# Second attention of a two-layer transformer: matmuls in the order written, rotation halves copied by ACT, one masked maximum for a row's last tile, and 28 instead of 17 units whose maxima DVE subtracts

## The chip, the cores and the metric

One core of a Trainium2 chip. The metric is the device time of one execution in microseconds. The five engines run independent queues, each in order: PE (TensorE, matmuls), DVE (VectorE), ACT (ScalarE), POOL (GpSimd) and SP (SyncE, which issues all DMAs here).

## The reference

Two layers, each attention and a mixture-of-experts FFN, on x of shape (2, 1024, 128), float32. The change lies in the second layer's attention, and a little in the FFN that follows. Shortened:

```
x = x + L0_attn(layernorm(x)); x = x + L0_ffn(layernorm(x))      # 16 heads of 8; 8 experts, top 2
h = layernorm(x)                                                  # second attention:
q = (h @ Wq) -> 8 heads of 128;  k = (h @ Wk), v = (h @ Wv) -> 4 heads of 128
q = q * cos + rotate_half(q) * sin;  k = k * cos + rotate_half(k) * sin
attn = softmax(where(causal, -inf, q @ k.T / sqrt(128)))          # two q heads share one kv head
x = x + (attn @ v).reshape(b, t, 1024) @ Wo
x = x + L1_ffn(layernorm(x))                                      # RMS norm inside, 16 experts, top 4
```

`rotate_half` puts the negated second half of the 128 head dimensions in front of the first half.

## The kernel before

The kernel runs five stages after one another on the one core: first attention (`attn0`), its FFN, second attention (`attn1`), its FFN (`ffn1_back`). The framework's scheduler orders each engine's instructions by a timeline it computes while building; only the first attention marks PE as scheduled by hand (`manual_schedule(engines={PE})`), which means that PE's queue is the order in which the program issues the matmuls.

The second attention works on 32 **units** (batch b, kv head, query chunk qc of 256 rows), numbered 16 b + 4 kv + qc. Three generators feed it:

- `attn1_proj` makes K, Q and V of one (b, kv): per half of 512 rows one K projection, two Q projections (three matmuls each, `mm3`, because values are split into a high and a low float32r part) and two V projections of six narrower matmuls (with Wo already folded in). K and Q pass through `rope`: DVE makes A = p * cos (`rA`) and the two halves of B = swapped p * sin (`rB`) straight from PSUM, POOL adds them, ACT casts the high part, POOL subtracts to get the low part.
- `attn1_s` finds the row maxima for the softmax ahead of its use: for each of a unit's two row tiles and two heads, PE makes scores `s` in tiles of up to 512 keys (PSUM pool `a1s`, three buffers). DVE reduces what lies wholly below the diagonal (`pm`, L838, and L840 where there are two tiles), then adds the causal mask to the last 128 columns and takes the maximum in the same instruction (L844). At the unit's end PE transposes the four columns of maxima (`mt`, L848). The maxima are rows now, and are taken off the transposed scores in one of two ways. For units in `APART` (17 of 32) ACT copies the rows, SP writes them to DRAM (`md`, L853) and reads them back broadcast to 128 partitions (`mb`, L854), and DVE subtracts (L883). For the others DVE builds `mr` (L859) and PE subtracts with a further matmul, the **row matmul** (L880).
- The main loop in `attn1` walks the units; a unit has 2 qc + 2 **steps** (kt), 20 for each (b, kv) and 160 in all. A step makes transposed scores `st` of 128 keys against 256 queries of both heads (three matmuls, L873; half as wide in a unit's last step), subtracts the maxima, takes the exponential on ACT into `pt` (L885, four buffers), and in a unit's last two steps POOL zeroes what lies above the diagonal (L889). Then `attn1_av` multiplies with V into `o` (L906; a 129th column of ones gives the softmax's sum). At the end of a row tile DVE takes the reciprocal (`rz`), ACT scales, POOL adds into x.

The loop issues the `o` of a step after the `st` of the next. `s` and projections are issued between, by fixed counts of steps (13 tiles of `s` ahead at the start, 28 for 20 steps; ten projections for 20 steps, all in the first twelve). `st`, projections, `mt` and other transposes share a PSUM pool of three buffers (`pt`). Side work (`Side`): layer norms and transposes of the second batch, weights of the last FFN, and `ffn1_front` (norm, gating, top-k) of chunks 0, 1 and 2, one generator step for each attention step.

Of the kernel before, what the change touches and what calls it, by code (L numbers as in the profile page):

```python
# [20 lines left out]
D = 128  # L21
# [3 lines left out]
CH = 512  # L25
# [8 lines left out]

APART = (3, 4, 6, 7, 12, 14, 15, 18, 21, 22, 24, 26, 27, 28, 29, 30, 31)
INV_SQRT_D = 1.0 / float(D) ** 0.5
# [36 lines left out]
class Net:  # L73
# [481 lines left out]
    def topk(self, sc, k, E, name):  # L555
        nc = self.nc
        n = sc.shape[1]
        idx = self.idx[:, 0:E].unsqueeze(1).to_broadcast([128, n, E])
        s1 = self.small.tile([128, n, 1], F32, tag="tk1", name=f"tk1_{name}")
        eq = self.small.tile([128, n, E], F32, tag="tk2", name=f"tk2_{name}")  # L560
        work = self.small.tile([128, n, E], F32, tag="tk3", name=f"tk3_{name}")
        sel = self.small.tile([128, n, E], F32, tag="tk4", name=f"tk4_{name}")
        first = self.small.tile([128, n, 1], F32, tag="tk5", name=f"tk5_{name}")
        for i in range(k):
            cur = sc if i == 0 else work
            m = first if i == 0 else s1
            nc.vector.tensor_reduce(m, cur, AX.X, ALU.max)
            nc.vector.tensor_tensor(eq, cur, m.to_broadcast([128, n, E]), ALU.is_equal)
            nc.vector.tensor_mul(eq, eq, idx)
            nc.vector.tensor_reduce(s1, eq, AX.X, ALU.max)  # L570
            nc.vector.tensor_tensor(eq, eq, s1.to_broadcast([128, n, E]), ALU.is_equal)
            if i + 1 < k:
                nc.vector.scalar_tensor_tensor(work, eq, -3.0e38, cur, ALU.mult, ALU.add)
            if i == 0:
                nc.vector.tensor_copy(sel, eq)
            else:
                nc.vector.tensor_add(sel, sel, eq)
            yield
        return sel, first
# [133 lines left out]
    def attn1_weights(self, ctx):  # L713
# [4 lines left out]
        self.sin = wp.tile([128, T], F32, name="sin")  # L718
        self.cmask = wp.tile([128, 128], F32, name="cmask")
        self.bmask = wp.tile([4, 4, 1], F32, name="bmask")  # L720
# [47 lines left out]
    def rope(self, dst, p, i, name):  # L768
        nc, wk = self.nc, self.a1r
        cs = cols(i, CH)  # L770
        A = wk.tile([128, CH], F32, tag="rA", name=f"rA_{name}", bufs=2)
        Bt = wk.tile([128, CH], F32, tag="rB", name=f"rB_{name}")
        nc.vector.tensor_mul(A, p, self.cos[:, cs])
        nc.vector.tensor_mul(Bt[0:64], p[64:128], self.sin[64:128, cs])
        nc.vector.tensor_mul(Bt[64:128], p[0:64], self.sin[0:64, cs])  # L775
        nc.gpsimd.tensor_add(A, A, Bt)
# [39 lines left out]
    def attn1_s(self, kvt, b, kv, qc, res):  # L816
# [3 lines left out]
        for t in range(2):  # L820
            qt = 2 * qc + t
            n = (qt + 1) * 128
            for h in range(2):
                col = m[:, 2 * h + t : 2 * h + t + 1]
                ini = -3.0e38
                for k0 in range(0, n, CH):
                    k1 = min(n, k0 + CH)
                    s = self.a1s.tile([128, CH], F32, tag="s", name=f"s_{b}_{kv}_{h}_{qt}_{k0}")
                    with ExitStack() as ctx:
# [4 lines left out]
                        )  # L834
                    w = min(n - 128, k1) - k0
                    if w > 0:
                        pm = self.small.tile([128, 1], F32, tag="pm", name=f"pm_{b}_{kv}_{h}_{qt}_{k0}")
                        nc.vector.tensor_reduce(pm, s[:, 0:w], AX.X, ALU.max)  # L838
                        if k0 > 0:
                            nc.vector.tensor_max(pm, pm, ini)  # L840
                        ini = pm
                    if k1 == n:
                        d = s[:, n - 128 - k0 : n - k0]
                        k = nc.vector.tensor_tensor_reduce(d, d, self.cmask, 1.0, ini, ALU.add, ALU.max, col)  # L844
                        self.marks["V"] = k
                    yield
        tp = self.pt([4, 128], f"mt_{b}_{kv}_{qc}")
        nc.tensor.transpose(tp, m, self.ident)  # L848
        if self.rows_apart(b, kv, qc):
# [5 lines left out]
            res[(b, kv, qc)] = mb  # L855
            yield
            return
        r = wk.tile([4, 4, 128], F32R, tag="mr", name=f"mr_{b}_{kv}_{qc}", bufs=3)
        nc.vector.tensor_mul(r, self.bmask.to_broadcast([4, 4, 128]), tp.unsqueeze(1).to_broadcast([4, 4, 128]))  # L859
        res[(b, kv, qc)] = r  # L860
        yield

# [58 lines left out]
    def attn1(self, first, first_gen, xh, side_plan):  # L921
# [23 lines left out]
        def s_stream():  # L945
            for b, kv, qc in units:
# [3 lines left out]
                yield from self.attn1_s(kvts[(b, kv)], b, kv, qc, mres)  # L950

        ps = proj_stream()
        next(ps)
        ss = s_stream()
        lead = 0
        lag = []
        step = 0
        for u, (b, kv, qc) in enumerate(units):
            for g in side_plan.get(u, ()):
                extra.add(g())  # L960
            kvt = kvts[(b, kv)]
            while (b, kv, qc) not in mres:
                next(ss)
                lead += 1
            mr = mres.pop((b, kv, qc))
            acc = {}
            for kt in range(2 * qc + 2):
                e = self.attn1_st(kvt, b, kv, qc, kt, mr)
                step += 1
                while lead < 13 + step * 28 // 20:  # L970
                    next(ss, None)
                    lead += 1
                k, r = divmod(max(step - 3, 0), 20)
                want = min(5, 2 * step) + 10 * k + (min(10, r * 10 // 12 + 1) if step >= 3 else 0)
                while sum(pdone.values()) - 5 < want:
                    if next(ps, 1) == 1:
                        break
                extra.step()
                lag.append((kvt, b, kv, qc, kt, e, acc))
                if len(lag) > 1:  # L980
                    self.attn1_av(*lag.pop(0))
        for args in lag:
            self.attn1_av(*args)
        extra.drain()

# [30 lines left out]

    def ffn1_front(self, c):
        nc = self.nc
        E = 16
        x = self.x[c]  # L1020
        assert self.nx[("a1", c)] == 16
        mv = yield from self.stats([x[:, t, :] for t in range(TPC)], f"f1_{c}")
        v = self.small.tile([128, 2 * TPC], F32, tag="f1v", name=f"f1v_{c}")
        nc.vector.tensor_scalar(v[:, 0:TPC], mv[:, :, 1], 1e-5, None, ALU.add)
        nc.vector.scalar_tensor_tensor(v[:, TPC:], v[:, 0:TPC], 1e-5, mv[:, :, 1], ALU.mult, ALU.add)
        rs = self.rsqrt(v, 2 * TPC, f"f1_{c}")
        yield
        xl = self.tok.tile([128, TPC, D], F32, tag="xl", name=f"f1xl_{c}")
        tt = self.tok.tile([128, TPC, D], F32, tag="xn", name=f"f1tt_{c}")
        for t in range(TPC):  # L1030
            for dst, j in ((tt, TPC + t), (xl, t)):
                nc.vector.tensor_scalar(
                    dst[:, t, :], x[:, t, :], mv[:, t, 0:1], rs[:, j : j + 1], ALU.subtract, ALU.mult
                )
            yield
        nc.gpsimd.tensor_add(x, x, xl)
        tp = self.pt([128, CH], f"f1tp_{c}")
        self.transposes(tp, tt)
        xT = self.tok.tile([128, CH], F32, tag="xT", name=f"f1T_{c}")
        nc.scalar.mul(xT, tp, self.f1sc)  # L1040
        yield
        xh = [self.hl.tile([128, CH], F32R, tag=f"fh{k}", name=f"f1x{k}_{c}", bufs=3) for k in range(2)]
        self.split(xh, xT)
        yield
        lg = self.pt([128, TPC, E], f"f1lg_{c}")
        for t in range(TPC):
            nc.tensor.matmul(lg[:, t, :], lhsT=xT[:, cols(t)], rhs=self.f1gw, start=True, stop=True)
        g = self.small.tile([128, TPC, E], F32, tag="f1g", name=f"f1g_{c}")
        nc.vector.tensor_add(g, lg, self.f1gb.unsqueeze(1).to_broadcast([128, TPC, E]))
        yield  # L1050
        sel, mx = yield from self.topk(g, 4, E, f"f1_{c}")
        nc.vector.tensor_sub(g, g, mx.to_broadcast([128, TPC, E]))
        nc.scalar.activation(g, g, AF.Exp)
        nc.vector.tensor_mul(g, g, sel)
        self.normalise(g, E, f"f1_{c}")
        yield
        gp = self.pt([E, CH], f"f1gp_{c}")
        self.transposes(gp, g)
        gT = self.hl.tile([E, CH], F32, tag="fgT", name=f"f1gT_{c}", bufs=3)
        nc.scalar.copy(gT, gp)  # L1060
        gd = self.dram.tile([E, CH], F32, tag="f1gd", name=f"f1gd_{c}", bufs=4)
        nc.sync.dma_start(out=gd, in_=gT)
        self.f1st[c] = (xh, gT, gd)
        yield

# [74 lines left out]
def build(tc, aps, upto=4):  # L1140
# [7 lines left out]
    with ExitStack() as ctx:  # L1148
# [35 lines left out]
        with ExitStack() as c2:  # L1184
            with ExitStack() as c3:
# [14 lines left out]
                if upto > 3:  # L1200
                    plan[9] = [lambda: held(n, weights1())]
                    plan[18] = [lambda: n.ffn1_front(0)]
                    plan[21] = [lambda: n.ffn1_front(1)]
                    plan[30] = [lambda: later(n.ffn1_front(2), 3)]
# [11 lines left out]
def layout(inputs):  # L1216
# [31 lines left out]
    o["cos"] = np.concatenate([np.cos(ang), np.cos(ang)], axis=1).T.astype(np.float32)  # L1248
    o["sin"] = np.concatenate([np.sin(ang), -np.sin(ang)], axis=1).T.astype(np.float32)
    o["cmask"] = np.triu(np.full((128, 128), -1.0e38, np.float32), 1)  # L1250
    o["bmask"] = -np.eye(4, dtype=np.float32)[:, :, None]
# [29 lines left out]
```

## Time and profile before

| what | value |
|---|---|
| runs | 969.1, 977.7, 968.48 us; median 969.1 |
| profiled execution | 963.49 us, its span 961.7 |
| PE clock granted, mean | 0.991 |
| busy in the span | PE 924.5, DVE 824.9, ACT 597.7, POOL 314.7 us |
| busy from 500 to 850 us (second attention) | PE 344.1, DVE 310.5, ACT 166.3 us |
| second attention, first `st` to last `o` | 469.5 to 847.6 us |

Busy time counts from an instruction's start to its end as the profile has them. Instructions of one engine overlap at their ends, matmuls most, so that a busy share near 100% doesn't say that nothing more fits. "Idle before ... <- X" in a line names what released the engine after it had waited. A name such as `pt<-st,mb` says which tile is written from which.

### The profile page before, as it was taken

The page shows a single profiled execution, that of the slowest core. Times are in us where ns is not written, and L with a number is a line of the kernel's source. Part 1 is how long each engine was busy: PE and PEld are TensorE (multiplying, and loading weights), DVE is VectorE, ACT ScalarE, POOL GpSimd, SP SyncE. Part 2 cuts the span into 40 slices and gives each one's busy share as a digit, 9 for nine tenths or more (in the row PEclk, how much of TensorE's full clock was granted, in tenths as well). Part 3 has the DMA queues.
Part 4 walks back from the last instruction along what each step waited for, and adds up shares of the span by engine and source line. Part 5 has one row for each costly group of instructions (what it writes and reads, how often), then busy time and mean ns, then how long its engine had stood idle before and what let it go on. Part 6 is the DMA issues. An engine that isn't in the chain of part 4 may idle for free.

```text
span 961.7 us, 17534 instructions
## 1 busy us (share of the span) xinstructions
PE 924.5 (96%) x6554; PEld 608.8 (63%) x6554; DVE 824.9 (86%) x1793; ACT 597.7 (62%) x1160; POOL 314.7 (33%) x392
## 2 busy tenths in 40 slices
PE   7999999999999999999899999999999999998997
PEld 4544444444444444567678888787878789876675
DVE  7998789989998989557688978899989898899986
ACT  3178788888887878853344455444445445577785
POOL 9002100000100000022564657364646365336332
PEclk8999999999999999999999999999999999999999
DMA  6620530011010000042000001000000000154462
GB/s 177 197 78 1 167 120 1 1 45 48 16 31 1 1 1 2 2 132 68 1 1 23 13 21 56 12 13 12 13 12 13 13 12 34 35 165 153 154 195 70
DMA packets 33127, 50.80 MB, mean 53 GB/s; under 512 B 4693, under 2 KB 10802, under 8 KB 33042
## 3 DMA queue, kind: packets, MB, share of 16 engines
q1 hardware_dynamic: 33042, 49.68, 16.2%
q8 instruction: 51, 0.84, 0.4%
q14 instruction: 34, 0.28, 0.1%
HBM read 40.00 MB, written 9.67 MB: 52 GB/s over the span
## 4 chain that ended last, share of the span: by engine, by line
PE 67%; DVE 19%; ACT 8%; issue 4%; POOL 0%; DMA 0%; DVEq 0%; ACTq 0%; POOLq 0%
PE av L427 12%; PE st L407 11%; PE o L906 9%; PE st L873 8%; ACT pt L413 3%; PE s L832 3%; PE st L880 3%; PE av L374 2%; PE f0y L702 2%; DVE mx L368 2%; DVE pm L838 2%; PE f1y L163 2%; PE hot L374 2%; DVE pt L883 2%; PE f1p L163 2%
## 5 line engine op out<-in xcount | busy, mean ns | idle before, releaser
L368 DVE TENSOR_REDUCE mx<-s 128x2 f32<-128x1024 f32 x256 | 300.3, 1218 | 28.4 <-PE s L363 23.8
L413 ACT ACTIVATE pt<-st 128x512 f32<-128x512 f32 x476 | 253.4, 602 | 43.6 <-PE s L363 33.9
L427 PE MATMUL av<-pt,V 128*32 128x256 f32 x2048 | 159.3, 392 | 0.0
L906 PE MATMUL o<-V,pt 128*128 128x129 f32 x1152 | 156.8, 277 | 0.7 <-ACT pt L885 0.7
L906 PEld LDWEIGHTS o<-V,pt 128*128 128x128 f32 x1152 | 146.8, 191 | 12.8 <-issue 3.9
L363 PE MATMUL s<-KS,QM 24*128 24x512 f32 x512 | 152.0, 496 | 2.1 <-DVE mx L368 1.6
L407 PE MATMUL st<-QX,KS 25*128 25x512 f32 x476 | 144.2, 495 | 3.8 <-ACT pt L413 2.3
L873 PE MATMUL st<-Q,K 128*128 128x512 f32 (+1 forms) x480 | 133.2, 389 | 4.9 <-DVE rB_q L775 3.4
L407 PEld LDWEIGHTS st<-QX,KS 25*128 25x128 f32 x476 | 63.0, 182 | 98.8 <-ACT pt L413 46.0
L456 POOL TENSOR_TENSOR x<-x,ov 128x128 f32<-128x128 f32 x16 | 7.3, 455 | 331.8 <-DVE ov L453 331.8
L885 ACT ACTIVATE pt<-pt 128x512 f32<-128x512 f32 x92 | 53.8, 592 | 73.4 <-DVE pt L883 73.4
L838 DVE TENSOR_REDUCE pm<-s 128x1 f32<-128x512 f32 (+3 forms) x160 | 80.7, 522 | 16.9 <-PE s L832 16.0
L873 PEld LDWEIGHTS st<-Q,K 128*128 128x128 f32 x480 | 78.8, 189 | 16.6 <-DVE rB_q L775 4.7
L427 PEld LDWEIGHTS av<-pt,V 128*32 128x32 f32 x2048 | 42.9, 108 | 63.5 <-issue 59.2
L885 ACT ACTIVATE pt<-st 128x512 f32<-128x512 f32 x68 | 37.5, 551 | 62.8 <-PE st L880 51.7
L363 PEld LDWEIGHTS s<-KS,QM 24*128 24x128 f32 x512 | 65.6, 182 | 10.4 <-DVE mx L368 6.7
L832 PE MATMUL s<-K,Q 128*128 128x512 f32 (+2 forms) x192 | 66.4, 379 | 2.8 <-DVE m L844 2.7
L919 POOL TENSOR_TENSOR x<-x,w 128x128 f32<-128x128 f32 x128 | 59.5, 465 | 24.7 <-ACT w L917 20.4
L883 DVE TENSOR_TENSOR pt<-st,mb 128x512 f32<-128x512 f32 x92 | 57.5, 631 | 5.0 <-PE st L873 1.5
L163 PE MATMUL f1y<-f1s,f1w 128*128 128x512 f32 x192 | 55.1, 406 | 5.8 <-POOL f1s L159 3.5
L917 ACT ACTIVATE w<-o,rz 128x128 f32<-128x128 f32 x128 | 39.9, 364 | 33.2 <-DVE rz L913 25.4
L889 POOL TENSOR_SCALAR_AFFINE_SELECT pt<-pt 128x256 f32<-128x256 f32 x64 | 26.4, 415 | 91.9 <-ACT pt L885 90.1
(228 smaller groups left out, 1594.1 us busy)
## 6 DMA issues: line engine op xcount, KB each, us to landing
f1gb<-f1gd SPq DMA_DIRECT2D x64, 256.0 KB
mb<-md SPq DMA_DIRECT2D x17, 256.0 KB
f0gb<-f0gd SPq DMA_DIRECT2D x32, 128.0 KB
kd<-k SPq DMA_DIRECT2D x12, 256.0 KB
qd<-q SPq DMA_DIRECT2D x12, 256.0 KB
QM<-qd SPq DMA_DIRECT2D x3, 1024.0 KB
KS<-kd SPq DMA_DIRECT2D x2, 1024.0 KB
KS<-kd SPq DMA_DIRECT2D x2, 768.0 KB
```

The source lines that it names most:

```text
L163: self.nc.tensor.matmul(out, lhsT=lhs[l], rhs=rhs[r], start=start and i == 0, stop=stop and i == 2)
L363: self.last_s = nc.tensor.matmul(ps[:, k, :], lhsT=QM[c][r, g, cols(t)], rhs=KS[c // 2][r, g, cols(h, CH)], start=True, stop=True)
L368: self.marks["V"] = nc.vector.tensor_reduce(mxs[n][:, h, 2 * pr : 2 * pr + 2, t : t + 1], ps, AX.X, ALU.max, negate=True)
L407: nc.tensor.matmul(ps, lhsT=KS[c // 2][32 * j : 32 * j + 25, g, cols(kt)], rhs=QX[n][32 * j : 32 * j + 25, :], start=True, stop=True,)
L413: self.marks["A"] = nc.scalar.activation(e, ps, AF.Exp, scale=INV_SQRT_D)
L427: return nc.tensor.matmul(avs[n][cols(j, 32), q], lhsT=V[c // 2][kt // 4][:, kt % 4, 4 * g + j, :], rhs=es[j][:, q], start=kt == 0 and i = ...
L832: nc.tensor.matmul(s[:, 0 : k1 - k0], lhsT=Q[0][:, h, cols(qt)], rhs=K[0][:, k0:k1], start=True, stop=True)
L838: nc.vector.tensor_reduce(pm, s[:, 0:w], AX.X, ALU.max)
L873: k = nc.tensor.matmul(o, lhsT=K[l][:, cols(kt)], rhs=Q[r][:, :, q0 : q0 + w], start=i == 0, stop=apart and i == 2)
L883: nc.vector.tensor_sub(e[:, :, 256 - w :], o, mv)
L885: k = nc.scalar.activation(e[:, :, 256 - w :], o, AF.Exp, scale=INV_SQRT_D)
L906: nc.tensor.matmul(acc[t][:, h, :], lhsT=e[:, h, cols(t)], rhs=V[:, kt, h, :], start=(kt == 0 and h == 0), stop=(kt == qt and h == 1),)
```

## The change

1. The second attention's matmuls are issued under `manual_schedule(engines={PE})`: PE's queue is the program's order. The transpose of a unit's maxima and what follows it move out of `attn1_s` into `attn1_rows`, which is called two steps after the unit's last `s` (`due1`), or at once when the unit's first step comes before that.
2. `rope`: ACT copies the two halves of the projection from PSUM into `rB`, exchanged; DVE then multiplies `rB` by a sine table with its signs changed, in one instruction and in place.
3. `attn1_s`: DVE reduces only whole tiles of 512 that another follows. The last tile of a row, 128 to 512 columns, is masked and reduced in one instruction, with a mask of 512 columns of which the right part is used.
4. `APART` becomes all units but every eighth (28 of 32): only the fourth chunk of the odd kv heads keeps the row matmul.
5. `ffn1_front` takes several chunks. Chunks 0 and 1 are done together, begun at unit 18 (before: at 18 and at 21).

```diff
-APART = (3, 4, 6, 7, 12, 14, 15, 18, 21, 22, 24, 26, 27, 28, 29, 30, 31)
+APART = tuple(u for u in range(32) if u % 8 != 7)
 ...
-        self.cmask = wp.tile([128, 128], F32, name="cmask")
+        self.cmask = wp.tile([128, CH], F32, name="cmask")
 ...
+        nc.scalar.copy(Bt[0:64], p[64:128])
+        nc.scalar.copy(Bt[64:128], p[0:64])
         nc.vector.tensor_mul(A, p, self.cos[:, cs])
-        nc.vector.tensor_mul(Bt[0:64], p[64:128], self.sin[64:128, cs])
-        nc.vector.tensor_mul(Bt[64:128], p[0:64], self.sin[0:64, cs])
+        nc.vector.tensor_mul(Bt, Bt, self.sin[:, cs])
         nc.gpsimd.tensor_add(A, A, Bt)
 ...
-                    w = min(n - 128, k1) - k0
-                    if w > 0:
-                        pm = self.small.tile([128, 1], F32, tag="pm", name=f"pm_{b}_{kv}_{h}_{qt}_{k0}")
-                        nc.vector.tensor_reduce(pm, s[:, 0:w], AX.X, ALU.max)
-                        if k0 > 0:
-                            nc.vector.tensor_max(pm, pm, ini)
-                        ini = pm
-                    if k1 == n:
-                        d = s[:, n - 128 - k0 : n - k0]
-                        k = nc.vector.tensor_tensor_reduce(d, d, self.cmask, 1.0, ini, ALU.add, ALU.max, col)
+                    if k1 < n:
+                        ini = self.small.tile([128, 1], F32, tag="pm", name=f"pm_{b}_{kv}_{h}_{qt}_{k0}")
+                        nc.vector.tensor_reduce(ini, s, AX.X, ALU.max)
+                    else:
+                        d = s[:, 0 : n - k0]
+                        mask = self.cmask[:, CH - (n - k0) :]
+                        k = nc.vector.tensor_tensor_reduce(d, d, mask, 1.0, ini, ALU.add, ALU.max, col)
                         self.marks["V"] = k
                     yield
+        self.due1[self.step1 + 2].append(lambda: self.attn1_rows(m, b, kv, qc, res))
+        yield
+
+    def attn1_rows(self, m, b, kv, qc, res):
+        nc, wk = self.nc, self.a1k
         tp = self.pt([4, 128], f"mt_{b}_{kv}_{qc}")
         nc.tensor.transpose(tp, m, self.ident)
 ...
+        def tick():
+            for f in self.due1.pop(self.step1, ()):
+                f()
+            self.step1 += 1
 ...
+        with self.tc.manual_schedule(engines={PE}):
 ...
                 while (b, kv, qc) not in mres:
-                    next(ss)
-                    lead += 1
+                    if self.due1:
+                        tick()
+                    else:
+                        next(ss)
+                        lead += 1
                 mr = mres.pop((b, kv, qc))
                 acc = {}
                 for kt in range(2 * qc + 2):
                     e = self.attn1_st(kvt, b, kv, qc, kt, mr)
 ...
+                    tick()
                     extra.step()
                     lag.append((kvt, b, kv, qc, kt, e, acc))
                     if len(lag) > 1:
                         self.attn1_av(*lag.pop(0))
 ...
-    def ffn1_front(self, c):
+    def ffn1_front(self, *cs):
 ...
-                    plan[18] = [lambda: n.ffn1_front(0)]
-                    plan[21] = [lambda: n.ffn1_front(1)]
+                    plan[18] = [lambda: n.ffn1_front(0, 1)]
 ...
-    o["sin"] = np.concatenate([np.sin(ang), -np.sin(ang)], axis=1).T.astype(np.float32)
-    o["cmask"] = np.triu(np.full((128, 128), -1.0e38, np.float32), 1)
+    o["sin"] = np.concatenate([-np.sin(ang), np.sin(ang)], axis=1).T.astype(np.float32)
+    o["cmask"] = np.triu(np.full((128, 512), -1.0e38, np.float32), 385)
```

## The prediction

> **What bounds the kernel now.** I read the page's first part, then the second attention alone (469.5 to 847.6 us, first score matmul `st` to last output matmul `o`), cut by windows at the eight (batch, kv head) pairs, then the costliest groups there, the timeline of a few steps, and last the order in which the built programs list each engine's instructions.
>
> ```profile
> PE 924.5 (96%) x6554; PEld 608.8 (63%) x6554; DVE 824.9 (86%) x1793; ACT 597.7 (62%) x1160; POOL 314.7 (33%) x392
> ```
> ```profile
> 469.50:523.50 54.00, 51.70 (x301) 41.13 (x302) 44.56 (x117) 23.97 (x49) 29.95 (x37) 1.00 0.03 11
> ...
> sum 378.10, PE 370.25 PEld 305.86 DVE 333.22 ACT 178.60 POOL 204.77; mean PE 46.28 PEld 38.23 DVE 41.65 ACT 22.33 POOL 25.60
> ```
> The columns are the stretch, its length, busy time (instructions) of PE, weight loads, DVE, ACT and POOL, PE's clock, and DMA. In these 378.1 us PE is busy 98%, DVE 88%, ACT 47%, POOL 54%. PE sets the end, DVE is close behind. Because matmuls overlap, I price PE by the distance from one start to the next. The chain of waits gives 0.70 for the three wide `st` matmuls (0.233 per 512 columns), 0.70 for a K or Q projection, 0.71 for a V projection, 0.89 for eight `o` records (0.11 each). The timeline gives the row matmul L880, which subtracts a unit's maxima on PE:
>
> ```profile
> 606.09 0.87 PE L873 MATMUL st<-Q,K 128*128 128x512 f32 x3
> 606.88 0.49 PE L880 MATMUL st<-mr,ones_r 4*128 4x512 f32 x1
> 607.30 0.50 PE L832 MATMUL s<-K,Q 128*128 128x512 f32 x1
> ```
> From `st` to what follows the row it is 1.21, so a wide row costs 1.21 - 0.70 = 0.51, a narrow one 0.12 less (379 against 494 ns in the groups), about 0.40. Priced so, everything PE does in the stage is st 101, o 127, s 33, projections 52, rows 33, the rest 6: 352 us. So PE loses only 26 of 378 us, although DVE is nearly full. The scheduler gets this by placing a step's `o` late: the median from last `st` (or row) matmul to first `o` is 4 to 5 us.
>
> The row path of a unit with subtraction on DVE is seen in the last unit, `st` being the step's scores:
>
> ```profile
> 830.37 0.27 PE L848 MATMUL mt<-ident,m 128*4 128x128 f32 x1
> 831.01 0.24 ACT L851 COPY mb<-mt 4x128 f32<-4x128 f32 x1
> 831.27 0.25 SPq L853 DMA_DIRECT2D md<-mb  x1
> 832.48 0.34 SPq L854 DMA_DIRECT2D mb<-md  x1
> 835.70 1.29 DVE L883 TENSOR_TENSOR pt<-st,mb 128x512 f32<-128x512 f32 x2 [0.42 <-DMA mb<-md]
> 836.42 1.29 ACT L885 ACTIVATE pt<-pt 128x512 f32<-128x512 f32 x2 [4.45 <-DVE pt L883]
> 836.45 1.68 PE L873 MATMUL st<-Q,K 128*128 128x512 f32 x6 [1.16 <-DVE pt L883]
> ```
> The transposed maxima go through DRAM and back: 5.33 us from `mt` to the subtraction, which the landing released (PE itself stood 1.16 us for it), and 6.7 to the end of the first exponential (836.42 + 0.63). Only then may that step's `o` run. In unit 12, where ACT was free, the copy came 0.31 after `mt` instead of 0.64, so the shortest is about 6.35.
>
> **The change: PE's rows.** 17 units become 28 with DVE subtraction. Rows fall from 53 wide and 15 narrow to 28 and 4: 25 x 0.51 + 11 x 0.40 = 17.2 us less PE work. All else on PE is the same in number, so the stage's PE work becomes 335.
>
> **DVE and ACT.** The groups in the stage:
>
> ```profile
> L883 DVE TENSOR_TENSOR pt<-st,mb 128x512 f32<-128x512 f32 x75 | 50.5, 680 | 4.0 <-PE o L906 1.2 <-PE mt L848 1.0 <-DMA mb<-md 0.8
> L838 DVE TENSOR_REDUCE pm<-s 128x1 f32<-128x512 f32 x64 | 43.6, 682 | 11.3 <-PE s L832 10.8
> L844 DVE CUSTOM_DVE_ANT_0 s<-s,cmask,pm 128x128 f32<-128x128 f32 x112 | 38.2, 348 | 2.4 <-PE s L832 1.6
> L775 DVE TENSOR_TENSOR rB_q<-qp,sin 64x512 f32<-64x512 f32 x30 | 20.5, 683 | 0.4
> L808 ACT COPY V<-vp 128x512 f32<-128x512 f32 x30 | 17.5, 585 | 9.5 <-PE vp L163 9.2
> L840 DVE TENSOR_TENSOR pm<-pm,pm 128x1 f32<-128x1 f32 x48 | 16.5, 347 | 0.3
> ```
> Removed from DVE: the 96 reductions of the last tile's unmasked part (17.4 + 13.3 + 8.7 = 39.4, the L838 groups of 384, 256 and 128 columns), L840 with 16.5, one of three rotation products (45 x 0.68 = 31), eleven `mr` products (11 x 0.67 = 7). Added: 25 x 0.68 + 11 x 0.42 = 21.6 for subtractions, and wider masked maxima. The trace has these at 128 columns only. They cost at least what they cost now (added 0) and at most that plus the reduction they replace (added 39); L838 grows by 0.13 per 128 columns, so 256, 384 and 512 columns add 0.13, 0.27 and 0.40, on average 0.20: 128 x 0.20 = 26. The merged FFN front saves some 6 (about 45 small instructions of 0.2, less what the wider ones cost).
>
> The remaining sine product reads two SBUF tensors, which none of the three does now. The nearest such row is L840: 159 ns in the median, 347 in the mean, 1256 at most, with long ones where POOL works. So the product is delayed by 0 to 1.1 us, and I take 0.19, L840's mean excess: 45 x 0.19 = 9. In sum DVE falls by 39 + 16.5 + 31 + 7 + 6 - 21.6 - 26 - 9 = 43, from 333 to about 290; with the bounds 265 to 345.
>
> The Trainium skill, "SBUF — State Buffer", section "SBUF: two separate sides", says that a DVE instruction with two SBUF inputs and a GpSimd instruction that reads SBUF lock each other out for the whole instruction. That speaks against moving the halves to SBUF: with POOL 54% busy in pieces of 1.28, an estimate by that rule is a delay of 0.54 x 0.64 = 0.35, or 16 instead of 9 on DVE, and the total would change by the 7 us only where DVE is what PE waits for.
>
> ACT gets 90 half copies in the stage at the price of L808 (0.585) and eleven copies of 0.24: 56 us, 179 to 235. That is hidden, since ACT had 200 us idle, except that it stretches the wait for an exponential. Without that cover it would cost up to 56. The eleven further units add 22 issues of 0.25 to 0.34 on SP, which has little else then. The wider mask is loaded before the stage.
>
> **PE in program order.** This decides it. In the new order step k's `o` always stands right behind step k+1's `st` and that step's `s` and projection. PE cannot go past it, so whatever a step's exponential is late by, PE stands still. And `mt` has moved: for 13 units with DVE subtraction (all eight of the third chunk, the fourth chunk of the even kv heads, and unit 1) the new list has `mt` immediately in front of the unit's first `st`. Between `mt` and that step's `o` the list holds, for the third chunk: st 0.70, s 0.23, V projection 0.71, two pairs of `o` records 0.44, st 0.70, s 0.41, V projection 0.71 = 3.9 us. The path needs 6.7. PE waits 2.8 in seven of these units; unit 30 has no projections left, 2.5 against 6.7, 4.2; the four fourth-chunk units have 3.55, wait 3.15 each; unit 1 has 3.0, wait 3.7. Sum 7 x 2.8 + 4.2 + 12.6 + 3.7 = 40. DVE, itself in order, holds its later work behind the late subtraction, and the two catch up together.
>
> Further waits: the first chunk's masked step has 1.3 us of PE work before its `o`, while the quicker masked steps of the trace need 2.3 (last `st` start to subtraction 0.46, 0.68, exponential 0.63, POOL's select 0.42, hand-overs): 7 x 1.0 = 7. The four row units have the row 0.73 behind `mt`, while the trace has `mr` done 1.0 to 1.5 behind it: 4 x 0.6 = 2.5. At the start `s` of the second half stands 2 us behind the Q projection it needs, whose rotation takes about 5 (hand-over 0.46, two copies 1.17, two products 1.55, POOL's add 1.28, cast 0.62), and the second head's is one POOL add behind: 4. New waits: 40 + 7 + 2.5 + 4 = 53.5.
>
> Against this, of the 26 that PE loses now, part goes because DVE is relieved. Bounds 0 and 26; I take half, 13.
>
> Sum: -17.2 + 53.5 - 13 = +23.3. The profiled execution took 963.5 (span 961.7 and 1.8 around it) and becomes 986.8. The median of the runs, 969.1, lies 5.6 above it: **992**.
>
> **Range.** Shortest path 6.35 takes 13 x 0.35 = 4.5 off the waits, row units 1.4 instead of 2.5, no start wait; all 26 recovered: -17.2 + 44 - 26 = +1. Longest: in the late units of the trace the subtraction starts 6.3 to 8.9 behind `mt`, some 1.4 more than 5.33: 13 x 1.4 = +18, nothing recovered: -17.2 + 53.5 + 18 = +54. The ends lie together only rarely; 8 in 10 is 972 to 1015.
>
> **Rivals.**
> (a) Faster. DVE is the real limit (the chain of waits of before runs through DVE from 631 to 640), and relief of 43 us lets the rows arrive early enough. Speaks for it: DVE 88% busy. Against: the late part is a DMA round trip, not DVE. If the 40 us of row waits stayed away: -17.2 + 13.5 - 26 = -30, 939. It decides below 20 us of new waits in all, a path of some 4.5 us. Chance 0.08.
> (b) No change: shortest path and everything now lost won back, +1: 970. Chance 0.14.
> (c) Much slower. In the second chunk's four steps DVE's list has four subtractions, three rotations with two products each, four reductions and four masked maxima: with three reciprocals 2.5 + 4.7 + 2.7 + 2.7 + 0.5 = 13 us against 8.5 of PE. If PE cannot use the following row wait to let DVE catch up, that is 8 x 2 to 3 more: 1012. Speaks against: the trace's starts lie 0.08 closer than these durations. Chance 0.19.
> The forecast itself: 0.59.
>
> A run of this kernel can tell about 1% from no change. Slower by more than that (over 979): 0.59 + 0.19 + 0.01 of (b), 0.79; within it 0.13; faster 0.08.
>
> **What would show it.** Right: the stage is about 400 us long, PE idle before `o` behind ACT's exponential some 50 us in total, in pieces of 2.5 to 4 us at each third chunk, with `mb<-md` as releaser of the subtraction; DVE's busy time there near 290. Wrong: the stage under 380, or `o` waiting evenly in all steps (then it is DVE or ACT, not the rows), or the masked maxima above 0.75 at 512 columns.

## The result and the profile after

The changed kernel takes **1045.7 us** (median of 4 runs, 1040.1 to 1048.3), the kernel before beside it 970.2. The ratio is 1.075, 95% interval 1.068 to 1.083: slower, as forecast, but by 75.5 us and not by 23, and 31 us above the upper end of the range.

The profiled execution took 1047.1 us against 963.5, 83.6 more. The second attention, from first `st` to last `o`, now runs from 473.8 to 930.1 us: 456.3 instead of 378.1, so 78.2 of the 83.6 lie there; 4.3 come before the stage, where half-clock spells (stretches in which the granted clock of PE is one half) stand in the first attention, and 1.2 behind it. The offset between execution and median that the prediction carried over, 5.6, goes with the clock: 0.991 in the profiled execution of before, 0.986 in the median of its runs. It did not carry over: the changed kernel's profiled execution lies 1.4 above its median. The page's first part, then the windows over the stage (456 us, columns as in the prediction):

```profile
PE 941.4 (90%) x6518; PEld 622.7 (60%) x6518; DVE 787.2 (75%) x1580; ACT 659.4 (63%) x1266; POOL 326.9 (31%) x392
```
```profile
sum 456.00, PE 379.31 PEld 314.35 DVE 298.97 ACT 236.37 POOL 215.67; mean PE 42.15 PEld 34.93 DVE 33.22 ACT 26.26 POOL 23.96
```
DVE fell from 333 to 299 and ACT rose from 179 to 236 (forecast 290 and 235). No engine is full any more: PE is busy 83% of the stage, DVE 66%. So most of the added time is not work, it is waiting. What PE waits for in the stage (total us, times, longest):

```profile
PE o L907 <- ACT pt L886: 37.8, 14, 5.8
PE o L907 <- POOL pt L890: 13.8, 19, 1.4
PE o L907 <- ACT w L918: 7.9, 9, 1.9
PE f1gp L167 <- DVE g_f L587: 6.8, 1, 6.8
```
In the kernel before the largest line of this view was this one:

```profile
PE st L873 <- DVE rB_q L775: 3.4, 7, 1.0
```
The first line of the changed kernel's view is the row path, by way of its exponential. A third chunk (unit 6) in the timeline; `mt` is the transpose of the maxima, `mb` the row tile:

```profile
554.03 0.27 PE L851 MATMUL mt<-ident,m 128*4 128x128 f32 x1
554.15 0.97 PE L874 MATMUL st<-Q,K 128*128 128x512 f32 x3
...
555.11 0.26 ACT L854 COPY mb<-mt 4x128 f32<-4x128 f32 x1
555.38 0.26 SPq L856 DMA_DIRECT2D md<-mb  x1
...
556.60 0.32 SPq L857 DMA_DIRECT2D mb<-md  x1
...
558.15 0.86 PE L163 MATMUL vp<-a1wvo,a1xT 128*128 128x256 f32 x6
559.93 1.29 DVE L884 TENSOR_TENSOR pt<-st,mb 128x512 f32<-128x512 f32 x2 [0.58 <-DMA mb<-md]
560.65 1.23 ACT L886 ACTIVATE pt<-pt 128x512 f32<-128x512 f32 x2
...
561.34 1.26 PE L907 MATMUL o<-V,pt 128*128 128x129 f32 x8 [2.33 <-ACT pt L886]
```
`mt` at 554.03, `st` right behind it, the subtraction 5.9 us later on the landing of `mb`, `o` at 561.34. PE stands 2.33 us, because in its list nothing is left ahead of `o`.

Priced by start-to-start distances as in the prediction, PE's own work in the stage is 335.2 us (forecast 335). The other 121 us are 58 waits of more than 0.35 us with 85.7 together, and 35.4 in small pieces. Before it was 14 waits with 9.5, and 16.4. That is the ledger: -17.0 for the rows, +76.2 for waits, +19.0 for small pieces = +78.2. The small pieces have a cause of their own, in the second part of the page (the clock in 40 slices, first before, then after):

```profile
PEclk8999999999999999999999999999999999999999
```
```profile
PEclk9999999999999989998999999999898999999999
```
In the stage nine spells of half clock, 44 us together, each following a long wait; before there was none there. Sorted by the clock, about 17 us of the small pieces lie outside the spells in either kernel, and the rest, 16 to 18 us, lies inside the nine.

### The profile page after: what moved, and what is told of

Its sections match the earlier page's. It is cut to its first block, busy times and chain, and to the rows that moved or that the text cites. A ratio compares the mean times of both kernels' runs of the same rounds, so it can differ in the third digit from the quotient of the medians.

```text
span 1045.4 us, 17504 instructions
## 1 busy us (share of the span) xinstructions
PE 941.4 (90%) x6518; PEld 622.7 (60%) x6518; DVE 787.2 (75%) x1580; ACT 659.4 (63%) x1266; POOL 326.9 (31%) x392
## 4 chain that ended last, share of the span: by engine, by line
PE 60%; ACT 13%; DVE 12%; issue 5%; POOL 5%; DMA 4%; SPq 0%; DVEq 0%; ACTq 0%; POOLq 0%
PE av L427 12%; PE st L407 10%; PE o L907 9%; PE st L874 6%; ACT pt L886 2%; DVE pt L884 2%; PE av L374 2%; ACT pt L413 2%; PE s L833 2%; PE f0y L702 2%; DMA mb<-md 2%; PE hot L374 2%; DVE mx L368 2%; PE f1p L163 1%; DVE f1f L1113 1%
## 5 line engine op out<-in xcount | busy, mean ns | idle before, releaser
L368 DVE TENSOR_REDUCE mx<-s 128x2 f32<-128x1024 f32 x256 | 300.5, 1219 | 32.4 <-PE s L363 26.3
L413 ACT ACTIVATE pt<-st 128x512 f32<-128x512 f32 x476 | 253.4, 602 | 46.6 <-PE s L363 33.7
L907 PE MATMUL o<-V,pt 128*128 128x129 f32 x1152 | 168.9, 287 | 59.7 <-ACT pt L886 37.8
L907 PEld LDWEIGHTS o<-V,pt 128*128 128x128 f32 x1152 | 153.9, 198 | 82.1 <-ACT pt L886 42.3
L874 PE MATMUL st<-Q,K 128*128 128x512 f32 (+1 forms) x480 | 145.8, 413 | 2.7 <-DVE rA_q L775 2.1
L886 ACT ACTIVATE pt<-pt 128x512 f32<-128x512 f32 (+1 forms) x128 | 73.9, 583 | 107.2 <-DVE pt L884 105.3
L884 DVE TENSOR_TENSOR pt<-st,mb 128x512 f32<-128x512 f32 (+1 forms) x128 | 79.3, 628 | 68.1 <-PE st L874 45.7
L890 POOL TENSOR_SCALAR_AFFINE_SELECT pt<-pt 128x256 f32<-128x256 f32 x64 | 31.3, 490 | 125.5 <-ACT pt L886 80.0
L1113 DVE SCALAR_TENSOR_TENSOR f1f<-f1f,f1gb 128x512 f32<-128x512 f32 x64 | 51.0, 813 | 7.9 <-ACT f1f L1112 6.8
L159 POOL TENSOR_TENSOR f1s<-f1f,f1s 128x512 fp32r<-128x512 f32 x24 | 38.7, 1612 | 57.3 <-ACT f1s L158 57.3
L163 PE MATMUL f1p<-f1x,f1w 128*128 128x512 f32 x192 | 53.5, 401 | 0.1
```

The costliest lines, as they stand in the source:

```text
L163: self.nc.tensor.matmul(out, lhsT=lhs[l], rhs=rhs[r], start=start and i == 0, stop=stop and i == 2)
L368: self.marks["V"] = nc.vector.tensor_reduce(mxs[n][:, h, 2 * pr : 2 * pr + 2, t : t + 1], ps, AX.X, ALU.max, negate=True)
L413: self.marks["A"] = nc.scalar.activation(e, ps, AF.Exp, scale=INV_SQRT_D)
L874: k = nc.tensor.matmul(o, lhsT=K[l][:, cols(kt)], rhs=Q[r][:, :, q0 : q0 + w], start=i == 0, stop=apart and i == 2)
L884: nc.vector.tensor_sub(e[:, :, 256 - w :], o, mv)
L886: k = nc.scalar.activation(e[:, :, 256 - w :], o, AF.Exp, scale=INV_SQRT_D)
```

## The experiments

The theory at the start (T): PE's order costs, by waits in its list and by half clock behind them. The rival (R): the other parts cost, the ACT copies, the DVE subtractions, the wide maxima.

### Which part costs

**The scheduler's order back**, all else of the change kept:
```diff
-        with self.tc.manual_schedule(engines={PE}):
+        if True:
```


> Changed kernel, all its parts kept (rotation halves by ACT, one masked maximum, 28 units subtracted by DVE, merged FFN front, maxima transposed two steps later), but TensorE's order in the second attention is chosen by the scheduler as in the kernel before. Theory T (the fixed order costs: some 39 us of row waits, 15 of masked steps, 10 of accumulator waits, 7 of the gate, 6 at the start, and about 19 of half clock behind these waits, against 17 won by the rows): nearly all of the 77 us comes back, 945 to 975 us, and the half-clock spells in the stage are gone. Rival R (the other parts cost: the copies on ACT, the late rows, the wider masked maxima): stays above 1000 us, with TensorE still waiting for exponentials about as long.

Measured: 994.4 us, ratio 1.025 (1.020 to 1.031). The order costs 51 us on top of the rest, but the rest is not a gain: 24 us slower than before. Neither theory had that.

**The order alone**, on the kernel before (with the maxima transposed two steps later, which comes with it):

> Kernel before with only TensorE's program order (and the maxima transposed two steps later) added; its 17 units with DVE subtraction, its rotation, its two-part maxima and its separate FFN fronts stay. T: six third-chunk units of the 17 wait for their rows (5 x 2.8 + 4.2 = 18), two fourth-chunk ones 6, fifteen row units 0.5 each = 7, masked steps 14, accumulators 10, start 6, half clock 10 to 19, nothing won by rows: 1030 to 1050 us. Rival R: under 990, since the parts that cost are not in it.

Measured: 1076.0 us, ratio 1.111 (1.106 to 1.116), above T's range and 30 us above the whole change. So units, rotation, maxima and front together are worth 30 us once the order is fixed. Its waits in the stage, and its clock:
```profile
PE o L909 <- ACT pt L888: 30.3, 13, 4.8
PE o L909 <- ACT w L920: 14.0, 16, 2.1
PE st L883 <- DVE mr L863: 7.4, 4, 2.4
```
```profile
PEclk8999999999999999988898988999898999889999
```
Counted as above, its waits over 0.35 us are 75 us together, fewer than the change's 85.7, so longer waits for a fuller DVE are not what makes it slower. What is longer is PE's own work (the 17 us of rows) and the half clock: 89 us of the stage run at it against 44, and the small pieces inside its spells are 37 us, some 21 more. Why its spells take up twice the time is not shown.

**The parts one at a time, in the scheduler's order.** First the 28 units alone:
```diff
-APART = (3, 4, 6, 7, 12, 14, 15, 18, 21, 22, 24, 26, 27, 28, 29, 30, 31)
+APART = tuple(u for u in range(32) if u % 8 != 7)
```


> Kernel before, TensorE's order still the scheduler's, with one edit: DVE subtracts the maxima in the 28 units of the change. Theory T1 (late rows cost under any order: the scheduler fixes each engine's order too, so a subtraction whose row has not landed holds everything behind it on DVE; 11.4 us of such waits stood in the changed kernel in the scheduler's order): DVE gets some 14 us more work and those waits, against 17 us off TensorE: 975 to 1000 us. Rival (only the fixed order of TensorE makes late rows cost): 950 to 962 us.

Measured: 989.8 us, 1.021 (1.018 to 1.024), in T1's range, but not for its reason. DVE waits for a landing of `mb` once, 1.3 us; PE waits for the maxima that a fuller DVE delivers late:
```profile
PE s L832 <- DVE m L844: 7.2, 7, 2.2
PE mt L848 <- DVE m L844: 5.3, 4, 2.0
```
Then the rotation and the maxima alone:
```diff
+        nc.scalar.copy(Bt[0:64], p[64:128])
+        nc.scalar.copy(Bt[64:128], p[0:64])
         nc.vector.tensor_mul(A, p, self.cos[:, cs])
-        nc.vector.tensor_mul(Bt[0:64], p[64:128], self.sin[64:128, cs])
-        nc.vector.tensor_mul(Bt[64:128], p[0:64], self.sin[0:64, cs])
+        nc.vector.tensor_mul(Bt, Bt, self.sin[:, cs])
...
+                        d = s[:, 0 : n - k0]
+                        mask = self.cmask[:, CH - (n - k0) :]
```


> Kernel before, TensorE's order still the scheduler's, with two edits: rotation halves exchanged by ACT, and one masked maximum per row's rest. Theory: DVE's 333 us in the stage fall by some 50 to about 285, ACT's 179 rise to about 235, and about half of the 26 us that TensorE loses there comes back: 950 to 965 us. Rival (the copies on ACT stand ahead of exponentials, and the sine product meets POOL): 975 us or more.

Measured: 968.9 us, ratio 0.998 (0.995 to 1.000): nothing, where the theory had 950 to 965. DVE's busy time in the stage did fall, from 333 to 292 us, and ACT's rose from 179 to 230; PE's stayed at 370. DVE's relief by itself is worth nothing in the scheduler's order.

Both together:

> Kernel before (TensorE's order the scheduler's, lead 13, maxima transposed as before, separate fronts) with 28 units subtracted by DVE, halves exchanged by ACT and one masked maximum. Theory (the 28 units alone cost 20 us because DVE, busier by 14 us, comes late with maxima and rows; the relief of DVE pays for itself only then): 968 to 980 us. Rival (late rows, not DVE's load, are what costs in the scheduler's order): 985 us or more.

Measured: **963.4 us**, ratio 0.994 (0.991 to 0.996), below the theory's range too. This beats both kernels: +20 for the units alone and -1 for the relief alone make -7 together. So what cost 20 was DVE's load; with the relief the PE waits for `m` shrink to 2.2 us and the rows taken off PE come through:
```profile
PE st L871 <- DVE pt L881: 6.0, 9, 1.6
PE o L904 <- ACT w L915: 2.9, 3, 1.5
PE mt L846 <- DVE m L842: 2.2, 1, 2.2
```
Between this and the first experiment (994.4) lie only the later transposes and the merged front. With the later transposes alone (and second buffers for three small tiles of the front's top-k):
```diff
+        self.due1[self.step1 + 2].append(lambda: self.attn1_rows(m, b, kv, qc, res))
```


> Changed kernel without program order on TensorE (the scheduler's) and with the two FFN fronts apart as before; of the change's parts it keeps the 28 units, the rotation, the masked maxima and the maxima transposed two steps later. Without the last part the same kernel took 963.4 us, with the merged front added as well 994.4. Theory D (the later transposes bring the rows late, and DVE's fixed list then holds everything behind the subtraction): 985 to 995 us. Rival M (the merged front is what costs): 960 to 968 us.

Measured: 987.5 us, ratio 1.019 (1.013 to 1.025). The two-step deferral costs 24 us in the scheduler's order. The merged front is the remaining 7, with intervals that overlap. From `mt` to its unit's first `st` the traces have 5.06 us before (median of the units whose maxima DVE subtracts), 6.14 in the kernel of 963.4, and 2.42 here, with 13 of 28 units under 2 us (2 of 28 without the deferral). DVE then holds its whole list for the landing:
```profile
DVE pt L884 <- DMA mb<-md: 13.4, 12, 2.5
```
**The deferral undone in the changed kernel**, PE still in program order (`self.step1 + 2` becomes `self.step1`):

> Changed kernel, TensorE in program order, with one edit: the maxima are transposed in the step in which their last score tile is reduced, and not two steps later. Theory (the later transposes are what makes rows late; in the scheduler's order they cost 24 us): the row waits go, 25 us as with constant rows, while the transposes now wait for DVE's last masked maximum, 0.3 to 0.8 us in each of 32 units, so 1030 to 1047 us. Rival (DVE has the maximum ready in time): 1015 to 1025 us. Rival (TensorE waits a whole DVE round at each transpose): above 1060 us.

Measured: 1026.8 us, ratio 1.058 (1.052 to 1.063), 19 us less than the change, just below the theory's range. `mt` to `st` is 6.28 us in the median, the waits for exponentials fall from 37.8 to 9.5, and transposes wait in their turn:
```profile
PE o L907 <- ACT w L918: 15.1, 16, 2.9
PE mt L851 <- DVE m L842: 9.8, 9, 1.6
```
**The old 17 units in the changed kernel:**

> Changed kernel, with only the old 17 units subtracted by DVE; TensorE in program order, relieved rotation and maxima, merged front kept. Theory (TensorE's order is what costs, and the kind of unit little): 11 units go back to row products, +17 us on TensorE, +5 of row-unit waits, -12 to -15 of row waits: 1045 to 1060 us. Rival (the 28 units are what costs): under 1025 us.

Measured: 1050.7 us, 1.087 (1.081 to 1.093), as the theory said: the kind of unit matters little once the order is fixed.

### Which wait binds in program order

**Rows earlier**, then **value products later**, then both:
```diff
-                    while lead < 13 + step * 28 // 20:
+                    while lead < 17 + step * 28 // 20:
...
-                    if len(lag) > 1:
+                    if len(lag) > 2:
```


> Changed kernel with the scores (and so the transposed maxima) running 17 instead of 13 steps ahead at the start, and so 2 to 3 steps more at each unit. T: the row waits (about 39 us) and the half clock behind them (10 of 19) go, the masked steps, accumulator and gate waits stay: 990 to 1005 us. Rival: DVE or ACT is the true bound and the waits only move to other steps: above 1030 us.

> Changed kernel with the value products two steps behind the scores products instead of one. T: each row wait shrinks by one step of some 2.2 us (13 units, 25 to 30 us), the masked steps' 14 us go, and half of the half clock with them: 990 to 1010 us; accumulator and gate waits stay. Rival: ACT or DVE is the true bound: above 1030 us.

> Changed kernel with both the longer lead (17) and the longer lag (two steps). Each alone took about 21 to 23 us off. Theory (they take away the same row waits in part, and accumulator and gate waits stay): 1003 to 1015 us. Rival (the two hide different waits): 990 to 1000 us. A third (another bound under both, DVE or ACT): 1020 us or more.

Measured: 1025.7, 1023.0 and 1006.6 us (ratios 1.060, 1.058, 1.038). Each alone came out 13 to 21 us above the theory's range; the third lies in its own. The row waits did go: with the lead the `o <- ACT pt` line is 1.8 us instead of 37.8. But only 20 us came back: two other lines grew, the masked steps (`o <- POOL pt`) from 13.8 to this,
```profile
PE o L907 <- POOL pt L890: 21.2, 24, 2.1
```
and the wait for the accumulator, which the next run shows as well.

**No row waits at all**: DVE subtracts a constant.
```diff
-            nc.vector.tensor_sub(e[:, :, 256 - w :], o, mv)
+            cv = self.cos[:, 0:512].rearrange("p (h q) -> p h q", h=2)[:, :, 256 - w :]
+            nc.vector.tensor_sub(e[:, :, 256 - w :], o, cv)
```


> Changed kernel in which DVE subtracts a constant table instead of the rows of maxima; the transposes, the copies and the DMAs of the rows are still made, but nothing waits for them (what is left out: the right maxima in the exponentials). Theory (the row path is the largest cost of the fixed order: about 39 us of TensorE waits and 10 to 13 of half clock behind them): 990 to 1000 us. Rival (the waits then stand in the next step of the same chain, subtraction, exponential, select): 1025 us or more.

Measured: 1020.9 us (ratio 1.053, 1.049 to 1.056), nearer to the rival. The row path is worth 25 us, though PE stood some 39 us for it. In its place stands the accumulator: each of a unit's two row tiles has one PSUM buffer for its `o`, and PE waits for ACT to empty it (`w`). This line in the changed kernel with the longer lead, with lead and lag, and with the constant:
```profile
PE o L907 <- ACT w L918: 20.7, 17, 3.3
```
```profile
PE o L907 <- ACT w L918: 26.3, 18, 4.2
```
```profile
PE o L908 <- ACT w L919: 23.4, 21, 3.9
```
It was 7.9 in the changed kernel. So this wait stood behind the row wait, and grew as that one went.

**A faster engine for it**: lead and lag, and DVE scales the accumulator in one product.
```diff
-                for h in range(2):
-                    nc.scalar.mul(w[:, h, :], acc[t][:, h, 0:128], rz[:, h, :])
+                nc.vector.tensor_mul(w, acc[t][:, :, 0:128], rz.to_broadcast([128, 2, 128]))
```


> Longer lead and lag as before, and the finished accumulator is scaled by one DVE product of 256 columns instead of two products on ACT. Theory (value products wait 26 us for ACT to empty the one accumulator, since ACT's list holds an exponential ahead of it; DVE's reciprocal stands right before): 20 us of them go, 980 to 990 us. Rival (DVE's list is late as well): 1000 us or more.

> The same with the two FFN fronts apart as in the kernel before. Theory (the merged front's gate transpose stands in TensorE's list 7 us before the normalisation ends, and its first transpose 4 us before its input): 8 to 11 us less than with the merged front, 970 to 980 us. Rival (each of two fronts then waits half as long, and DVE gets 45 small instructions back): no difference.

Measured: 1007.9 and 1009.4 us, against 1006.6 without these edits. Nothing from either, although DVE's one product takes 0.42 us and ACT's two took 0.36 each: the wait is now for DVE and about as long.
```profile
PE o L907 <- DVE w L917: 23.7, 21, 3.6
```
**More room in the list**: lead and lag, ACT as before, but the first products of a unit's second accumulator stand one step later.
```diff
+        todo = [(t, kt, e) for t in range(2) if kt <= 2 * qc + t]
+        if kt == 0:
+            acc["held"] = todo.pop(1)
+        elif kt == 1:
+            todo.insert(len(todo) - 1, acc.pop("held"))
```


> Longer lead (17) and lag (two steps), and the first value products of a unit's second accumulator stand one step later, so that two steps instead of one lie between a unit's last use of that accumulator and the next unit's first; nothing else. Theory S (the waits stand behind one another: with the rows early, the single accumulator is the next to bind, and more time in the list, not a faster engine, takes it away): the 20 to 26 us of waits for the accumulator go, 980 to 990 us. Rival (in program order the throughput of DVE or ACT binds, whichever wait is named): 1000 us or more.

> The same, and the gate transposes of the merged front stand three steps later in TensorE's list, the transposes of the second batch's normalised input two steps later. Theory S: another 8 to 11 us, 970 to 981 us. Rival (these waits only take the place of others that would come): no difference to the kernel without this.

Measured: 991.9 us (1.023, 1.019 to 1.026) and, with the two transposes moved as well, 986.9 (1.019, 1.015 to 1.023). The accumulator line falls from 26.3 to 8.0, and 15 us come back:
```profile
PE o L910 <- ACT w L921: 8.0, 9, 1.5
```
Theory S, waits one behind the other, is upheld, a little short in size: a faster engine did nothing, a place one step later did. Moving the two transposes brought only 5 us, with intervals that overlap; the gate's still waits 7.8 us for DVE's normalisation three places further on. Why is open. Of the 17 us that this last kernel still lacks to the one before, the clock would be some 10 to 12, by the price in the next part (28.6 us of lost clock against 13.6; an estimate). In its profiled execution 11 us of small pieces lie in half-clock spells and 42 us are waits over 0.35 us, against none and 9.5 before; so the 17 us of rows are still outweighed by waits.

**The longer lead in the scheduler's order**, on the kernel of 963.4:

> The same with the longer lead (17 instead of 13), so that rows land 2 to 3 steps earlier. Theory (DVE relieved and rows early: the 17 us of row products off TensorE stay won): 948 to 960 us, below the kernel before. Rival (something else then binds, as in program order): 966 us or more.

Measured: 972.3 us, ratio 1.002 (0.999 to 1.005), slower than with lead 13, as the rival said. There rows were hardly late: one landing of `mb`, 1.5 us, held DVE with lead 13. From `mt` to `st` the median goes from 6.14 to 14.5 us; why that costs 9 us is not shown.

### What the half clock costs

**Filling the row waits with spare matmuls:**
```diff
+                if t == 0 and (qc == 2 or (qc == 3 and kv % 2 == 0) or (b, kv, qc) == (0, 0, 1)):
+                    for _ in range(8):
+                        nc.tensor.matmul(o, lhsT=kvt[0][0][:, 0:128], rhs=kvt[0][0][:, 0:512], start=True, stop=True)
```


> Changed kernel with eight spare matmuls of 512 columns (1.9 us at full clock) ahead of the first value product of the 13 units in which TensorE waits for the row; their results are overwritten. Theory (the row waits also cost by the half clock behind them, eight windows of 3.4 us, some 12 us): the waits look filled, the half-clock windows behind them go, 1033 to 1042 us. Rival (the half clock costs nothing, TensorE waits as long as the others need): 1045 us or more.

Measured: 1046.1 us (6 runs), no difference. The waits were filled (`o <- ACT pt` 37.8 to 11.7), but the clock did not rise: 0.965 against 0.963 in the median. In the profiled execution the stage has four spells instead of nine, but one of them, near its end, lasts 24 us. It begins in a wait of 3.5 us for POOL's select (898.5 to 902.0) and goes on while PE no longer idles (columns as above; the clock is the number behind POOL's):
```profile
905.00:910.00 5.00, 5.00 (x13) 2.85 (x12) 1.15 (x6) 1.70 (x4) 0.91 (x2) 0.50 0.00 0
910.00:915.00 5.00, 5.00 (x18) 3.82 (x18) 0.00 (x0) 0.71 (x2) 0.00 (x0) 0.50 0.00 0
915.00:920.00 5.00, 5.00 (x17) 3.72 (x17) 0.00 (x0) 0.60 (x1) 0.00 (x0) 0.50 0.00 0
```
So this run does not tell what the idling in the row waits costs. The price can be had otherwise, since every run lists span and clock. Call (1 - clock) x time the lost clock. The six runs here go from 1038.4 us at 0.975 (26.0 lost) to 1048.6 at 0.961 (40.9): 0.68 us for each us lost. Over all 99 runs of changed kernels, each taken against its own kernel's mean, the slope is 0.79 (correlation 0.91); over 75 runs of the kernel before, 0.66. (A slope alone does not say that the clock is the cause, since longer waits lower the clock too; the 16 to 18 us of small pieces inside the spells say it independently.) The change loses 38.7 us in the median, the kernel before 13.6: 25 more, at 0.66 to 0.79 **17 to 20 us** of the 75.

## Why the prediction was wrong in size

**PE's rows, DVE, ACT: right.** PE's own work fell by 17.0 (forecast 17.2). The sizes bounded from far rows hold:
```profile
L842 DVE CUSTOM_DVE_ANT_0 s<-s,cmask,pm 128x512 f32<-128x512 f32 x16 | 12.0, 749 | 0.1
L842 DVE CUSTOM_DVE_ANT_0 s<-s,cmask,pm 128x128 f32<-128x128 f32 x16 | 5.6, 352 | 3.5 <-PE s L833 3.4
L776 DVE TENSOR_TENSOR rB_q<-rB_q,sin 128x512 f32<-128x512 f32 x30 | 26.5, 883 | 0.9 <-ACT rB_q L774 0.9
L776 DVE TENSOR_TENSOR rB_k<-rB_k,sin 128x512 f32<-128x512 f32 x15 | 11.2, 744 | 0.0
L775 DVE TENSOR_TENSOR rA_q<-qp,cos 128x512 f32<-128x512 f32 x30 | 20.5, 683 | 5.0 <-ACT rB_q L774 4.3
```
A masked maximum of 512 columns takes 0.749 where one of 128 takes 0.352: 0.13 per 128 columns, as taken. The sine product from two SBUF tensors averages 0.838 (37.7 us over 45), 0.15 over the cosine product's 0.684, so 7 us in all: the row's 9 was nearer than the 16 estimated by the rule of the Trainium skill's "SBUF — State Buffer", section "SBUF: two separate sides". DVE's lower bound, given as 265, comes to 255 by the prediction's own terms (nothing added for masks or for the delay); the measured 299 lies inside with either.

**The new waits: right, one by one.** The prediction asked 40 for the row waits: some 24 in the third chunks, 11.5 in the fourth chunks of the even heads and 3.4 in unit 1 make 39. It asked 7 for the masked steps of the first chunk: 7 times 1.0. Start 4: 5.6. Row units 2.5: 1. Together 52.6 against 53.5.

**The term that failed is "I take half, 13"**, the part of the 26 us that PE lost before and was to win back, with bounds 0 and 26. It came out as a loss of 42.6, and that is the whole miss (23.3 + 13 + 42.6 - 0.7 = 78.2). It had two parts. Waits not in the list: 33 us, against 9.5 before, so +23.6: the one accumulator (10 with its weight loads), the third chunks' masked steps (7.5), the merged front's gate transpose (7), the rest in `st` and projections. And the small pieces, +19.0, nearly all of it half clock: 16 to 18 us of them lie inside the nine spells, and the runs' clocks give 17 to 20.

The term's premise failed by itself too: with DVE relieved by 41 us and nothing else changed, the time stayed at 968.9, so no part of the 26 came back. And the bounds were wrong before the value was. Nothing excluded a loss there: a fixed list can wait at each of its places, and the prediction worked out those places where it had looked (the first product of a unit, the masked step of the first chunk) and booked the remainder as a saving. The run with the order alone has a larger remainder still: 56 us in small pieces, 37 of them at half clock.

**What the forecast could not separate** is that program order and deferral act on each other. Ledger by runs: 970.2 before; -7 for units, rotation and maxima together; +24 for the deferral; +7 for the front; +51 for the order; 1045.7. In this sequence 24 of the 75 us are not PE's order at all. Another sequence divides them otherwise, since the parts act on each other: order and deferral come to +106 on the kernel before, and the deferral to 19 once the order is fixed. The prediction noted that `mt` had moved next to `st`, but priced it only as a wait of PE; in the scheduler's order too, DVE holds its list for the landing (13.4 us).

**Removing waits gives less than their sum.** The 39 us of row waits were worth 25 without rows, since the accumulator's wait stood behind them.

**The rivals.** (a), DVE the real limit: its relief alone gave nothing that can be measured; with the 28 units it is what turns +20 into -7. The gain existed, in the order that was given up. (b), all won back: not seen. (c), DVE's list binding in the second chunk, with 2 to 3 us more in each third chunk's wait: not seen. Five of the eight third chunks wait 2.5 us (forecast 2.8); DVE is idle 157 us of 456, and waits for PE's scores longest.

## What to carry to other kernels

A fixed order turns every place in the list into a possible wait: list all places where an instruction can come before its operand, PSUM buffers and side work included, and never book the remainder as a gain. Try the parts of a change in the scheduler's order first; here three of them together are worth 7 us, and the fixed order, the deferral and the merged front turn that into a loss of 75. When the waits you name are gone and the time is not, look for the one that stood behind them, and give it room in the list before you give it a faster engine.

## What the runs showed of the hardware

TensorE's clock falls to one half in spells whose lengths are multiples of 3.41 us, on one fixed grid through an execution. Divide the stage by this grid into windows of 3.41 us and take the share of each that PE's matmul records cover. In the changed kernel all 11 windows under 45% are followed by a half-clock window, in the first experiment all 6, and over the 20 kernels all 107. Between 45 and 60% both occur (none of 8 in the changed kernel, 33 of 117 over all kernels); of some 2100 windows at full clock above 60%, one is. How long a spell lasts is not explained by this: in the kernel with spare matmuls one ran through seven windows that PE's records fill to 76 to 100%. If the 45% holds, a wait of 2.4 us costs clock or not by where it falls in the grid; that would be why the times of one kernel scatter with its clock (a slope of 0.66 to 0.79 us per us of lost clock).

The Trainium skill, "TensorE: Matmul & The Clock Gate", Part 1, gives a free-running window of 3413 ns, which the grid here agrees with, and says that for modelling the ramp costs under 1% of a typical span. That is said of the ramp when activity begins; here the spells recur behind waits. The 38.7 us of lost clock at 0.66 to 0.79 are 2.4 to 2.9% of the changed kernel, and the difference between the kernels about 2%. So an edit that adds waits of 2 us to PE should be priced with a clock term beside the waits.
